# A graph-attention stack: new rows stored from ScalarE's queue, and eleven buffers for the mask rows

## The chip, the cores and the metric

The kernel runs on one core of a Trainium2 chip. Its time is the device time of one execution in microseconds (us). The engines are PE (TensorE, matmul), DVE (VectorE), ACT (ScalarE), POOL (GpSimd) and SP (SyncE, which here only issues DMAs). ACT and POOL can issue DMAs too; the profile writes SPq and ACTq for the queues.

## The reference

Four graph-attention layers work on 3327 nodes with 512 features, over one adjacency matrix with few neighbours per node. Each is preceded by a layer norm and a relu, and added to its input:

```
h = relu(layernorm(x))
v = h @ W                                   # per head
e[i, j] = leaky_relu(s1[i] + s2[j], 0.2)    # s1, s2: scores, linear in v
alpha = softmax over the neighbours j of i
x = x + (alpha @ v)                         # layers 1 and 2: elu(...) first
```

The layers have 8, 4, 1 and 8 heads. The neighbours of a node are the same in all layers.

## The kernel before

The nodes are padded to 3328, 26 tiles of 128. A first stage (until the first gather of layer 0, at 273.46 us) reads the adjacency matrix, makes for every node a list of its neighbours, and ranks the nodes by their number, so that tile 0 has the nodes with the most neighbours (up to 36) and tile 25 those with the fewest (up to 11). The tables idx and twice say, for each tile and each k, the row of the k-th neighbour.

Each layer then has a table in DRAM with one row of 528 numbers per node: v and the scores. Layer 0 reads tabx; layers 1, 2 and 3 read tabs[1], tabs[0], tabs[1], which the layer before fills. In the profile these are all "tab".

**Gathered tiles (class Tile).** Tiles run from 25 down to 0. For each k, an indirect DMA of POOL (gather, L835) brings 128 neighbour rows into a buffer g; four of them make a group, and seven groups can be in flight (LOOK, gpool). For a group, scored adds the scores on DVE (z, L888 and L890) and takes the exponential on ACT (pw, L891); in layer 0 ACT also turns the neighbours' numbers into ranks (idx, L894). group multiplies on DVE (m, L917) and adds up on PE against the identity (bank, L922); with one head, in layer 2, DVE does both (L912). When a tile is complete its row goes through means, added, centre, root, turn, cut, project: DVE, ACT, PE and again PE (pv, L469). Last comes rows: ACT scales the result into v (L476, three buffers), and a DMA stores v in the next layer's table (L993). The pieces of one tile are spread over the steps of the following tiles by later(step, place, piece). The orders of POOL, PE, DVE and ACT are as written; that of SP is chosen by a scheduler when the program is built.

**Dense tiles.** The first tiles have many neighbours, so from layer 1 on they are computed densely, with masks of the adjacency: one tile in layer 1 and two in layer 3 (class Several), nine in layer 2 (class Wholes). These load rows of the table and of the masks through SP (L1230 and L1231 in Several, L1099 and L1101 in Wholes).

**Masks.** The masks are made in layer 0. Mask gathers the adjacency rows of the nine first tiles, turns them on PE, and keep stores them in the DRAM tensor found (L1041), whose rows are in the nodes' old order. Ranked(j), one for each of 26 tiles, brings them into rank order: POOL gathers 128 rows of found, 288 words each, into an SBUF buffer (L835), and SP stores the buffer in masks (L1061). Eight of these stand between the last eight steps of layer 0, and 18 after them. Their buffers are parts of spare, a tile of the first stage that nothing else in layer 0 uses:

```
rows = spare[:, self.j % 3 * n:(self.j % 3 + 1) * n].bitcast(I32)
gather(rows, found, slots(self.j, 0))
```

low, also a tile of the first stage (128 x 3328 words), holds a gathered adjacency row block for Mask earlier in layer 0, and is divided among the buffers of Several (a, e, b, c, v, mk, s) in layers 1 and 3; Wholes uses parts of it in layer 2.

The first gather of a layer waits for all 26 stores of its table.

Of the kernel before, what the change touches and what calls it, by code (L numbers as in the profile page):

```python
# [13 lines left out]
I32 = mybir.dt.int32  # L14
# [4 lines left out]
P = 128  # L19
# [18 lines left out]
ND = max(DENSE)  # L38
# [435 lines left out]
def scaled(nc, pv, rstd, work):  # L474
    v = work.tile([P, ROW], F32, name="v", bufs=3)
    nc.scalar.activation(v.rearrange("p (s n) -> p s n", s=2), pv[:, :, :ROW // 2], AF.Copy, scale=rstd)  # L476
    return v
# [319 lines left out]
def tile_gat_lists(ctx: ExitStack, tc: tile.TileContext, x, adj, ws, avs, out, ident, half, slots, L, low, spare, tabx, tabs):  # L797
# [7 lines left out]
    nc = tc.nc  # L805
# [26 lines left out]
    L, low, spare = [t.rearrange("p a b -> p (a b)") for t in (L, low, spare)]  # L832

    def gather(out_, table, which):
        nc.gpsimd.indirect_dma_start(out=out_, out_offset=None, in_=table,  # L835
                                     in_offset=bass.IndirectOffsetOnAxis(ap=which, axis=0))
# [3 lines left out]
    def scatter():  # L840
        while waiting:
            dst, t, rows = waiting.pop(0)
            nc.gpsimd.indirect_dma_start(out=dst, out_offset=bass.IndirectOffsetOnAxis(ap=slots(t, 0), axis=0),
                                         in_=rows, in_offset=None)

    class Tile:
# [10 lines left out]
        def fetch(self):  # L857

            l, t = self.l, self.t
            i = len(self.groups)  # L860
            k0 = self.k0[i]
            n = (self.k0 + [CAPS[t]])[i + 1] - k0
            g = gpool.tile([P, GROUP, ROW], F32, name="g")
            for q in range(n):
                if l > 0 and k0 + q == 0:
                    nc.sync.dma_start(g[:, 0, :], tabs[l % 2][t * P:(t + 1) * P, :])
                elif l > 0:
                    gather(g[:, q, :], tabs[l % 2], slots(t, k0 + q))
                elif k0 + q == self.own:
                    gather(g[:, q:q + 2, :].rearrange("p q n -> p (q n)"), tabx, slots(t, 0))  # L870
                else:
                    gather(g[:, q, :], tabx.rearrange("r (s n) -> (r s) n", s=2),
                           slots(t, k0 + q + (k0 == 0), twice=True))
            self.groups.append((k0, n, g))
# [115 lines left out]
        def rows(self):  # L990
            if self.W is not None:
                v = scaled(nc, self.pv, self.rstd, work)
                nc.sync.dma_start(tabs[(self.l + 1) % 2][self.t * P:(self.t + 1) * P, :], v)  # L993

        def ends(self, s):

# [54 lines left out]
    class Ranked:  # L1051
# [3 lines left out]
            self.j, self.k0 = j, [0]  # L1055

        def fetch(self):
            n = ND * P // 4
            rows = spare[:, self.j % 3 * n:(self.j % 3 + 1) * n].bitcast(I32)
            gather(rows, found, slots(self.j, 0))  # L1060
            nc.sync.dma_start(masks[:, self.j, :, :].rearrange("s p c -> p s c"),  # L1061
                              rows.rearrange("p (s c) -> p s c", c=wide // 4))
# [269 lines left out]
    for l in range(NL):  # L1332
# [3 lines left out]
        with ExitStack() as c2:  # L1336
# [39 lines left out]
            for s in range(-1, at_end):  # L1376
# [10 lines left out]
                if 0 <= s < len(steps):  # L1387
                    tl, i = steps[s]
# [55 lines left out]
```

## Time and profile before

| | |
|---|---|
| median of 3 runs | 3037.67 us (3028.95 to 3050.73) |
| the profiled execution's own time | 2485.15 us |
| its span, first to last instruction | 2483.4 us |
| busy: PE, DVE, POOL, ACT | 84%, 78%, 69%, 37% |
| granted TensorE clock, mean | 0.944 |
| DMA moved | 599.55 MB, 241 GB/s |
| layer 0, gathers of its own rows | 273.46 to 889.34 us |
| layer 1, first gather | 939.12 us |
| layer 2, first gather | 1495.78 us |
| layer 3, first gather | 1957.66 us |

The profiled execution is 552.5 us shorter than the median of the runs. Durations in this document are those of the profiled execution.

In the lines of the profile "out<-in xN" is N instructions that read "in" and write "out", by the program's names; a group of waits gives us in total, times, longest. A row of the table of stretches gives the length of the stretch, the busy time and number of instructions of PE, PEld (weight load), DVE, ACT and POOL, the granted clock of PE, the DMA engines' mean busy share, and GB/s. A row in order of time gives start, duration, engine, line, operation, tiles, and in brackets the idle time before it and what ended it.

### The profile page before, as it was taken

How to read it: one execution, taken by the hardware profiler on the slowest of the kernel's cores; microseconds unless marked ns; L12 is line 12 of the kernel's file. 1: busy time of each engine (PE TensorE's matmuls, PEld its weight loads, DVE VectorE, ACT ScalarE, POOL GpSimd, SP SyncE). 2: the span in 40 equal slices, each digit the busy share in tenths (PEclk: the TensorE clock that was granted, in tenths of full speed). 3: DMA queues.
4: the chain of work that ended last, by engine and by line, in shares of the span. 5: the costliest groups of instructions: out<-in, count | busy, mean ns of one | idle time of the engine just before them, and what ended most of it. 6: DMA issues, size and time to landing. Idle time of an engine off the chain costs nothing. (4 is left out here: it accounts for less than half of the span.)

```text
span 2483.4 us, 26799 instructions
## 1 busy us (share of the span) xinstructions
PE 2077.1 (84%) x6832; PEld 1161.7 (47%) x6832; DVE 1935.1 (78%) x5004; ACT 910.9 (37%) x2506; POOL 1709.5 (69%) x1700
## 2 busy tenths in 40 slices
PE   3778699999988846999999986869696699999897
PEld 1666345454444423555555543444353454455453
DVE  7988787887777725888888867978979488787776
ACT  4777024343321102434333323433333444333330
POOL 7898467777777756776777746655545377777775
PEclk9888899999999977999999998989898899999999
DMA  6796579999987878887888858867776488888885
GB/s 229 300 304 236 174 240 283 298 289 293 275 269 235 232 182 243 263 248 227 247 259 258 253 150 272 268 197 250 209 227 204 141 254 246 247 249 248 242 242 173
DMA packets 262490, 599.55 MB, mean 241 GB/s; under 512 B 103923, under 2 KB 121331, under 8 KB 257974
## 3 DMA queue, kind: packets, MB, share of 16 engines
q0 software_dynamic: 126128, 438.08, 58.6%
q1 hardware_dynamic: 132454, 152.86, 19.1%
q10 hardware_dynamic: 3744, 6.82, 0.8%
q8 instruction: 55, 0.90, 0.1%
q14 instruction: 109, 0.89, 0.1%
HBM read 547.96 MB, written 49.65 MB: 241 GB/s over the span
## 5 line engine op out<-in xcount | busy, mean ns | idle before, releaser
L922 PE MATMUL bank<-m,ident 128*128 128x512 f32 x2608 | 1202.3, 607 | 131.9 <-DVE m L917 131.2
L917 DVE TENSOR_TENSOR m<-g,pw 128x512 f32<-128x512 f32 x1304 | 810.7, 681 | 138.2 <-ACT pw L891 133.2
L835 POOL DMA_INDIRECT g<-tab,idxb x734 | 697.8, 951 | 281.7 <-issue 170.7
L922 PEld LDWEIGHTS bank<-m,ident 128*128 128x128 f32 x2608 | 482.7, 193 | 711.8 <-issue 345.2
L469 PE MATMUL pv<-w,hT 128*128 128x264 f32 x1664 | 439.0, 419 | 71.0 <-ACT hT L458 41.7
L891 ACT ACTIVATE pw<-z 128x32 f32<-128x32 f32 (+5 forms) x434 | 84.0, 194 | 987.8 <-DVE z L890 987.5
L469 PEld LDWEIGHTS pv<-w,hT 128*128 128x128 f32 x1664 | 336.5, 206 | 173.2 <-ACT hT L458 48.3
L835 POOL DMA_INDIRECT g<-tabx,twiceb x342 | 324.0, 947 | 104.4 <-issue 77.1
L835 POOL DMA_INDIRECT g<-tab,idxa x297 | 283.0, 953 | 148.0 <-issue 81.3
L1138 PE MATMUL whole<-ve,em 128*128 128x512 f32 x468 | 222.0, 623 | 41.0 <-DVE em L1124 38.9
L888 DVE TENSOR_TENSOR z<-g,pw 128x32 f32<-128x32 f32 (+5 forms) x434 | 75.0, 173 | 195.8 <-DMA g<-tab,idxa 88.4
L695 POOL TENSOR_TENSOR key<-a,keys 128x3328 int32<-128x3328 int32 (+1 forms) x29 | 189.4, 6536 | 16.6 <-DVE cand L704 12.9
L912 DVE SCALAR_TENSOR_TENSOR bank<-g,pw,bank 128x512 f32<-128x512 f32 x243 | 183.2, 754 | 6.8
L1138 PEld LDWEIGHTS whole<-ve,em 128*128 128x128 f32 x468 | 90.5, 199 | 151.1 <-issue 91.8
L704 DVE MAX8 cand<-key 128x8 f32<-128x208 int32 x416 | 143.8, 364 | 0.1
L835 POOL DMA_INDIRECT g<-tabx,twicea x99 | 94.4, 954 | 69.6 <-issue 31.3
L451 PE MATMUL pt<-ident,xn 128*128 128x128 f32 x416 | 68.8, 292 | 84.5 <-ACT hT L458 30.9
L451 PEld LDWEIGHTS pt<-ident,xn 128*128 128x128 f32 x416 | 54.3, 150 | 121.5 <-issue 49.4
L1113 ACT ACTIVATE r<-low,mc,b 128x384 f32<-128x384 f32 x78 | 52.6, 674 | 150.1 <-DVE em L1124 115.7
L1247 ACT ACTIVATE r<-low,spare 128x256 f32<-128x256 f32 x208 | 98.9, 476 | 5.1
L432 POOL TENSOR_TENSOR rstd<-ve,half 128x1 f32<-128x1 f32 x52 | 31.9, 615 | 94.8 <-DVE ve L975 60.4
L890 DVE SCALAR_TENSOR_TENSOR z<-z 128x32 f32<-128x32 f32 (+5 forms) x434 | 78.7, 181 | 15.2 <-DVE z L888 0.2
(175 smaller groups left out, 2113.6 us busy)
## 6 DMA issues: line engine op xcount, KB each, us to landing
a<-in_adj SPq DMA_DIRECT2D x25, 1664.0 KB
tab<-v SPq DMA_DIRECT2D x78, 264.0 KB
ve<-tab SPq DMA_DIRECT2D x78, 264.0 KB
g<-tab SPq DMA_DIRECT2D x66, 264.0 KB
tabx<-vx SPq DMA_DIRECT2D x26, 528.0 KB
g<-tab,idxb POOLq DMA_INDIRECT x734, 3.9
low<-tab SPq DMA_DIRECT2D x52, 132.0 KB
room<-tab SPq DMA_DIRECT2D x52, 132.0 KB
```

Of the source, the lines that this page charges most:

```text
L451: nc.tensor.transpose(pt[:, k, :], xn[:, k * P:(k + 1) * P], ident)
L469: nc.tensor.matmul(pv[:, s, :HF + 8], hT[:, k, :], W.w[:, k, s, :], start=(k == 0), stop=(k == KC - 1))
L695: nc.gpsimd.tensor_tensor(key[:, c:c + quarter], a[:, c:c + quarter], keys[:, c:c + quarter], OP.mult)
L704: nc.vector.max(cand[:, g * 8:(g + 1) * 8], key[:, g * SEG:(g + 1) * SEG])
L835: nc.gpsimd.indirect_dma_start(out=out_, out_offset=None, in_=table, in_offset=bass.IndirectOffsetOnAxis(ap=which, axis=0))
L890: nc.vector.scalar_tensor_tensor(z, z, SLOPE, z, OP.mult, OP.max)
L891: nc.scalar.activation(self.wt[:, k0:k0 + n, :H], z, AF.Exp)
L912: nc.vector.scalar_tensor_tensor(acc, v, w, acc, OP.mult, OP.add)
L917: nc.vector.tensor_tensor(m[:, q, :].rearrange("p (s h d) -> p s h d", s=2, d=D), v.rearrange("p s (h d) -> p s h d", d=D), wt[:, k0 + q, ...
L922: nc.tensor.matmul(self.po, ident, m[:, q, :], start=(k0 + q == 0), stop=(k0 + q == K - 1))
L1138: nc.tensor.matmul(tl.po.rearrange("p (s m) -> p s m", s=2), e[:, q * P:(q + 1) * P], v.rearrange("p (s m) -> p s m", s=2)[:, :, :F // 2], ...
L1247: nc.scalar.activation(self.r[:, h, :], self.a[:, g, :], AF.Relu, bias=-1.0, scale=self.b[:, j, g:g + 1])
```

## The change

The store of the new rows is issued by ScalarE instead of SP. The buffers of Ranked are parts of low instead of spare: low has room for 3328 // 288 = 11 of them, where there were three.

```
         def rows(self):
             if self.W is not None:
                 v = scaled(nc, self.pv, self.rstd, work)
-                nc.sync.dma_start(tabs[(self.l + 1) % 2][self.t * P:(self.t + 1) * P, :], v)
+                nc.scalar.dma_start(tabs[(self.l + 1) % 2][self.t * P:(self.t + 1) * P, :], v)
...
         def fetch(self):
-            n = ND * P // 4
-            rows = spare[:, self.j % 3 * n:(self.j % 3 + 1) * n].bitcast(I32)
+            n, many = ND * P // 4, low.shape[1] // (ND * P // 4)
+            i = self.j % many
+            rows = low[:, i * n:(i + 1) * n].bitcast(I32)
             gather(rows, found, slots(self.j, 0))
             nc.sync.dma_start(masks[:, self.j, :, :].rearrange("s p c -> p s c"),
                               rows.rearrange("p (s c) -> p s c", c=wide // 4))
```

## The prediction

> **What bounds the kernel now.** I read the busy line of the page first, then the table of stretches, then the waits by engine, then the instructions in order of time around the one place where both edits meet: the end of layer 0.
>
> ```profile
> PE 2077.1 (84%) x6832; PEld 1161.7 (47%) x6832; DVE 1935.1 (78%) x5004; ACT 910.9 (37%) x2506; POOL 1709.5 (69%) x1700
> ...
> 800.00:890.00 90.00, 77.85 (x200) 37.15 (x201) 59.61 (x148) 14.01 (x50) 68.06 (x73) 0.96 0.82 226
> ...
> 1300.00:1400.00 100.00, 100.00 (x319) 55.16 (x318) 86.90 (x230) 37.97 (x115) 75.62 (x81) 1.00 0.86 260
> ...
> 910.00:915.00 5.00, 0.00 (x0) 0.00 (x0) 0.00 (x0) 0.00 (x0) 2.83 (x3) 0.54 0.66 168
> ```
>
> In the steady stretches POOL issues 81 gathers in 100 us, one per 1.25 us (0.95 busy, 0.30 issue): it is never idle, and layers 0, 1 and 3 go at its pace, PE close behind. The last row is different: from 910 to 935 us PE, DVE and ACT do nothing. That hole is the boundary between layers 0 and 1, and the longest wait of DVE is in it:
>
> ```profile
> DVE z L888 <- DMA g<-tab,idxa: 88.4, 15, 41.5
> ...
> 888.39 0.95 POOL L835 DMA_INDIRECT g<-tabx,twiceb  x1 [0.30 <-issue]
> 889.64 0.94 POOL L835 DMA_INDIRECT spare<-found,idxb  x1 [0.30 <-issue]
> 894.04 0.94 POOL L835 DMA_INDIRECT spare<-found,idxb  x1 [3.46 <-DMA masks<-spare]
> ...
> 929.16 0.95 POOL L835 DMA_INDIRECT spare<-found,idxa  x1 [0.52 <-issue]
> 939.12 0.94 POOL L835 DMA_INDIRECT g<-tab,idxa  x1 [9.01 <-DMA tab<-v]
> ...
> 932.98 0.53 SPq L993 DMA_DIRECT2D tab<-v  x1
> ...
> 869.99 0.70 ACT L476 ACTIVATE v<-pv,rstd 128x528 f32<-128x528 f32 x1 [3.42 <-PE pv L469]
> 872.31 0.20 ACT L891 ACTIVATE pw<-z 128x32 f32<-128x32 f32 x1 [1.63 <-DVE z L890]
> ...
> 896.25 0.18 ACT L891 ACTIVATE pw<-z 128x8 f32<-128x8 f32 x1 [2.71 <-DVE z L890]
> ...
> 906.38 0.70 ACT L476 ACTIVATE v<-pv,rstd 128x528 f32<-128x528 f32 x1 [3.92 <-PE pv L469]
> ```
>
> Layer 0's last own gather goes at 888.39. 19 mask gathers follow; with three buffers each third waits for a store of the masks' rows, so they take 889.64 to 930.1 where 19 x 1.25 = 23.8 us would do. The last new row is ready at 907.08, but its store stands on SP behind the masks' stores and leaves at 932.98. Layer 1's first gather is let go at 939.12.
>
> **What the Trainium skill says.** "DMA: Bandwidth & Descriptors", section "Issuing engines are not separate DMA queues": transfers of all issuing engines end on the same 16 DMA engines, so another queue saves only issue time. By that page, moving the stores gives no bandwidth; what moves is who waits. "Two DMAs through the same engine are not ordered" says that order comes from the completion semaphore, for which the issuing engine waits. The trace agrees in effect: 69 waits of SP for v, 441.8 us in all. The same page, "Anatomy of one DMA": a fixed cost of about 2 us that is mostly completion. Here a tab store took 2.9 and 3.1 us from issue to the gather that needs it at the other two boundaries (1492.91 to 1495.78, 1954.55 to 1957.66). "TensorE: Matmul & The Clock Gate", Part 1, says the clock halves when PE idles and returns with work; the granted clock is 0.54 and 0.50 in the hole above.
>
> **The change, part by part.** PE, DVE and POOL keep their instructions in the same order, save that 26 gathers write low instead of spare. SP loses 78 stores, ScalarE gains 78, each right after its v. The waits that the changed program gives these stores decide the sum. All direct DMAs, of SP and ScalarE alike, take their completion semaphores from one set of eight, and each waits until the last user of its semaphore has completed. For a store now on ScalarE that user is mostly a transfer of SP, and ScalarE stands in order behind the wait.
>
> 1. *Eleven buffers.* The gathers need not wait in threes: 889.64 + 19 x 1.25 = 913.4 for the first gather of layer 1, if its table is there. That alone would be 939.12 - 913.4 = 25.7 us. DMA share in 890 to 935 us is 0.49 to 0.88, 29 us of full share in 45; compressed it fits barely, so up to 4 us of it may come back as slower landings.
>
> 2. *The second-last tab store waits for the eighth masks store.* Its v is ready at 870.7. The eighth mask gather is issued at 889.64 by POOL, which does not depend on ScalarE here (the buffers it needs were read before 870). Its two predecessors took 5.8 and 7.1 us from gather to store; its own store left at 895.3 in the trace, and the next stores completed in 2.7 to 3.1 us: done at 898 to 900, I take 899. So ScalarE is held from 870.7 to 899, and behind it stand the five remaining exponentials of layer 0 (872.31 to 896.25), for which DVE and then PE wait.
>
> 3. *The catch-up.* 17 rows (4+4+4+4+1) remain. PE takes 7.03 us for 16 matmuls at full clock, so 34 take 15; with 2.5 us for a halved clock at the start it ends at 899.5 + 17.5 = 917. From PE's end to the end of the last v the trace has 8.3 us (898.74 to 907.08), plus the wait before: v at 926.
>
> 4. *The last tab store waits for the last masks store*: gather 26 at 912.1, stored 3.2 to 7 us later and complete 3 us after that, 919 to 922. That is before 926 and costs nothing; it would decide if step 3 were 5 us faster.
>
> 5. Store at 926.1, landing 3.0: the first gather of layer 1 at 929.1 instead of 939.12. **Gain 10 us** (7 if it lands as slowly as the 6.1 us of before, 13 if PE keeps its clock). SP's part behind it (scores, values, masks of layer 1) waits for the same store, so DVE starts earlier by the same amount; POOL has seven groups of lookahead, and layer 1 moves as a whole.
>
> 6. *ScalarE's cost.* A direct DMA on its queue takes 0.334 us (the x loads of the first stage): 78 x 0.334 = 26 us, and up to 0.2 more each for its own v to end. ScalarE waits 2.6 us on average before its exponentials in layer 1 (290.5 us in 110 waits), so most is covered. Bounds: 0 and 42 us; I take 2, at layer ends.
>
> 7. *Other waits on shared semaphores.* In layers 1 and 2 nearly every store waits for an SP load. By the program's order that load stands 81 to 442 instructions earlier, and a layer has 5.7 to 7.2 per us: 14 us or more, against 3.3 to 6.3 us for a load to land. The exception, the last store of layer 1, waits for a small score load issued some 10 us before it (1480 to 1484, against 1492.9). I take 0; bounds 0 and 52 us (1 us each for 52).
>
> 8. *SP freed.* Loads no longer stand behind v. Only ScalarE's wait for ve (11.6 us in 6) shows loads late; three of them, 5.2 us, stand near a tab store. Gain 0 to 5, I take 1. The other two boundaries gain nothing: SP issued those stores 0.03 us after v.
>
> Sum: -10 + 2 - 1 = -9 us. Profiled execution: 2485.15 - 9 = 2476. The median of the runs shown is 3037.67, 552.5 us above the profiled execution, and nothing in the profile says where these lie. The gain carries over as 9 us, or as 11 if everything stretches alike. I predict 3028.
>
> **Rivals.**
> - *A, the above*, 50 in 100: 3028, own range 3013 to 3045.
> - *B, the full gain*: ScalarE isn't held at the eighth masks store (v comes later in unprofiled runs, or the catch-up is faster), and the whole 25.7 us stay: 2459 profiled, 3012 by difference, 3006 in proportion. For it: POOL's pure pace. Against it: the waits of step 2, which the program contains. 18 in 100, half of it beyond 1%.
> - *C, more*: if the missing 552.5 us are longer round trips, the ring of three costs more there: 19/3 rounds of 12 instead of 6 us is 76 us against about 30, a gain of 45: 2993. Against it: unknown. 14 in 100.
> - *D, slower*: one mechanism, ScalarE held in layers 1 and 2 by semaphores of SP loads, with z, exponential and product behind it. At 1 us for each of 52 stores it is 52 - 9 = +43: 2528 profiled, 3081. It cancels the gain from 0.17 us each and passes 1% from 0.75. For it: ScalarE is in every group's chain. Against it: step 7. 18 in 100.
>
> **How the numbers follow.** About 1% (30 us) is what a measurement of this kernel tells from no change. Faster: 9 of B, 14 of C, 2 of A make 0.25. Slower: 16 of D and 1 of A make 0.17. The rest is 0.58. The range, 2990 to 3065, holds A, B and nearly all of C, and leaves out most of D.
>
> **What would show it.** In the changed profile: mask gathers 1.25 us apart; ScalarE idle from about 870 to 899 between v and its store, with PE idle beside it; layer 1's first gather near 929; no wait over 1 us ahead of a store in layers 1 and 2. The forecast is wrong if ScalarE passes the second-last store at once (then B) or if DVE's waits for pw grow by tens of us in layers 1 and 2 (then D).

## The result, and the profile after

The changed kernel takes 3047.23 us (median of 14 runs, 3037.62 to 3062.81), the kernel before beside it 3025.88 us (14 runs): a ratio of 1.007, 95% interval 1.0048 to 1.0091. It is slower by 21 us; the forecast was 3028 us, with a gain of 9.

The kernel before took 2487 us in two of the five sets of runs below (the first kind) and 2993 to 3055 us in the other three (the second kind); within a set its executions lie within 1.7% of each other, and each set ran on a chip of its own. The profile that the prediction read was of the first kind, the runs of this comparison of the second. The profile of the changed kernel is of the second kind too (3058.75 us, span 3057.0), so it is read against a second profile of the kernel before, e0_before (span 3040.1). From the page of the changed kernel, its busy line and the chain that ended last, by engine:

```profile
PE 2252.4 (74%) x6832; PEld 1233.5 (40%) x6832; DVE 1930.9 (63%) x5004; ACT 918.0 (30%) x2506; POOL 1714.2 (56%) x1700
...
PE 35%; DVE 18%; issue 16%; another core or an unknown queue 12%; ACT 8%; DMA 6%; POOL 3%; ACTq 0%; DVEq 0%; SPq 0%; POOLq 0%
```

POOL is busy 56% of the span, not 69%: it no longer sets the pace. 12% of the chain lies behind a releaser that the profile cannot name. The same appears among the waits of the changed kernel (us in all, times, longest):

```profile
POOL g L835 <- issue: 491.7, 1305, 16.1
...
DVE m L917 <- ACT pw L891: 340.2, 171, 28.7
...
ACT v L476 <- remote: 119.7, 9, 30.0
```

"remote" is a wait for which no instruction or transfer ended at the right time. DVE's longest wait for an exponential was 4.5 us in the profile that the prediction used; here it is 28.7, and it stands at the place that the prediction spoke of (e0_before has one of 24.0 us, but in layer 3). Instructions of POOL, PE, ACT and DVE there, in order of time, in the changed kernel:

```profile
1069.77 0.21 ACT L894 ACTIVATE idxb<-g 128x4 int32<-128x4 f32 x1
1070.54 0.95 POOL L835 DMA_INDIRECT g<-tabx,twiceb  x1 [0.30 <-issue]
1071.48 3.72 PE L469 MATMUL pv<-w,hT 128*128 128x264 f32 x16
1071.80 0.95 POOL L835 DMA_INDIRECT low<-found,idxb  x1 [0.30 <-issue]
1073.05 0.95 POOL L835 DMA_INDIRECT low<-found,idxb  x1 [0.30 <-issue]
...
1094.88 0.95 POOL L835 DMA_INDIRECT low<-found,idxa  x1 [0.85 <-issue]
1100.02 0.70 ACT L476 ACTIVATE v<-pv,rstd 128x528 f32<-128x528 f32 x1 [30.04 <-remote]
1100.75 0.33 ACTq L993 DMA_DIRECT2D tab<-v  x1
1101.36 1.88 DVE L917 TENSOR_TENSOR m<-g,pw 128x512 f32<-128x512 f32 x3 [28.71 <-ACT pw L891]
...
1134.20 0.95 POOL L835 DMA_INDIRECT g<-tab,idxa  x1 [38.37 <-DMA tab<-v]
```

The 19 mask gathers that follow layer 0's own now go without a break, from 1071.80 to 1094.88, as forecast. But ScalarE is not held at the second-last store: that leaves at 1100.75, as soon as its v has ended. All 78 stores of this profile leave 0.03 us after their v. It is v itself that comes 30 us late, although PE's product for it ended near 1075.2. In e0_before, with the ring of three:

```profile
1065.70 0.95 POOL L835 DMA_INDIRECT spare<-found,idxb  x1 [0.30 <-issue]
1067.86 0.95 POOL L835 DMA_INDIRECT spare<-found,idxb  x1 [1.21 <-DMA masks<-spare]
1073.40 0.95 POOL L835 DMA_INDIRECT spare<-found,idxb  x1 [4.60 <-DMA masks<-spare]
...
1077.03 0.70 ACT L476 ACTIVATE v<-pv,rstd 128x528 f32<-128x528 f32 x1 [6.34 <-PE pv L469]
...
1114.62 0.95 POOL L835 DMA_INDIRECT g<-tab,idxa  x1 [8.27 <-DMA tab<-v]
```

POOL has to stop for stores, for 4.60 us among others, and v follows PE's product at once. Two stretches of 25 us among the mask gathers, first of the changed kernel, then of e0_before (columns as in the prediction):

```profile
1075.00:1100.00 25.00, 3.64 (x9) 1.34 (x8) 0.00 (x0) 0.00 (x0) 15.41 (x17) 0.62 0.71 189
```

```profile
1080.00:1105.00 25.00, 21.18 (x55) 10.81 (x54) 13.77 (x39) 4.07 (x13) 11.37 (x12) 0.93 0.59 157
```

With eleven buffers PE ends its last 3.6 us of work and then POOL works alone; DVE and ACT do nothing for 25 us. With three, PE, DVE and ACT finish layer 0 under the mask gathers.

An engine that has finished an instruction raises a counter, its completion semaphore, and an engine that needs the result waits for a count. The trace records when TensorE's counter rises, and that shows what "remote" is here. In e2_buffers (below), where PE's product for v ended near 1076.9 and v waits from 1072.5 to 1102.85, the rises are at 1080.22, 1085.83, and then at 1102.83, 1102.87, 1102.91, 1102.95 and 1103.00: two completions come through singly during the row of gathers, and five at once 5 us after the last mask gather ended. v waits for one of them. Its only other wait was for a store three rows earlier, and that had landed at 978.9. The Trainium skill, "Perfetto Trace Analysis", section "Tensor Engine Instruction (MATMUL, LD_WEIGHTS)", says that the end of a matmul in a profile is an estimate, and that the update of the semaphore is pushed, and then made known to all engines, after it. The trace agrees that the two differ: here by some 26 us.

Such bursts (two rises or more within 0.06 us of each other) are 117 in e0_before and 103 in the changed kernel, and 4 in the profile that the prediction read. The larger ones were taken from seven traces with gathers 1.25 us apart (four rises or more after over 3 us without one, 9 to 30 gathers in an unbroken row ahead): 129 of them. Each comes after a stop of POOL, 2.8 to 6.3 us after the last gather was issued, and the later the longer the row: a straight line gives 1.82 us + 0.139 us for each gather of the row (correlation 0.94). It looks as if each gather took 1.39 us of something, while POOL issues one every 1.25 us, and as if TensorE's signals came through only when the backlog is worked off.

### The profile page after: what moved, and what is told of

It is laid out like the page before. It is cut to its first block, busy times and chain, and to the rows that moved or that the text cites. A ratio compares the mean times of both kernels' runs of the same rounds, so it can differ in the third digit from the quotient of the medians.

```text
span 3057.0 us, 26770 instructions
## 1 busy us (share of the span) xinstructions
PE 2252.4 (74%) x6832; PEld 1233.5 (40%) x6832; DVE 1930.9 (63%) x5004; ACT 918.0 (30%) x2506; POOL 1714.2 (56%) x1700
## 4 chain that ended last, share of the span: by engine, by line
PE 35%; DVE 18%; issue 16%; another core or an unknown queue 12%; ACT 8%; DMA 6%; POOL 3%; ACTq 0%; DVEq 0%; SPq 0%; POOLq 0%
PE bank L922 23%; PE pv L469 7%; DVE m L917 6%; DVE bank L912 3%; POOL g L835 3%; DMA vx<-in_x 3%; PE whole L1282 2%; ACT r L1248 1%; PE pi L786 1%; ACT v L476 1%; DMA g<-tab,idxa 1%; DVE prod L409 1%; ACT pw L891 1%; PE whole L1139 1%
## 5 line engine op out<-in xcount | busy, mean ns | idle before, releaser
L922 PE MATMUL bank<-m,ident 128*128 128x512 f32 x2608 | 1330.1, 658 | 353.9 <-DVE m L917 223.1
L917 DVE TENSOR_TENSOR m<-g,pw 128x512 f32<-128x512 f32 x1304 | 811.1, 682 | 573.5 <-ACT pw L891 340.2
L922 PEld LDWEIGHTS bank<-m,ident 128*128 128x128 f32 x2608 | 529.7, 211 | 1015.2 <-issue 629.5
L476 ACT ACTIVATE v<-pv,rstd 128x528 f32<-128x528 f32 x78 | 54.1, 694 | 291.6 <-remote 119.7
L1259 ACT ACTIVATE spare<-room,low 128x64 f32<-128x64 f32 x208 | 57.8, 336 | 201.7 <-remote 101.1
L458 ACT ACTIVATE hT<-pt 128x512 f32<-128x512 f32 x104 | 61.4, 590 | 143.9 <-PE pt L451 42.5
L1282 PE MATMUL whole<-spare,low 128*128 128x130 f32 x416 | 67.3, 301 | 48.1 <-issue 47.9
```

The source lines that it names most:

```text
L917: nc.vector.tensor_tensor(m[:, q, :].rearrange("p (s h d) -> p s h d", s=2, d=D), v.rearrange("p s (h d) -> p s h d", d=D), wt[:, k0 + q, ...
L922: nc.tensor.matmul(self.po, ident, m[:, q, :], start=(k0 + q == 0), stop=(k0 + q == K - 1))
L1282: nc.tensor.matmul(dst, e[:, h, q * P:(q + 1) * P], mov, start=False, stop=(j == NT - 1), skip_group_check=True)
```

## The experiments

Theories at the start: H, ScalarE held at its stores by shared semaphores in all layers; B, only the hold at the end of layer 0; M, the eleven buffers cost. From the second set on, W: TensorE's signals don't come through while gathers follow one another, and the ring of three was what broke their row.

**First set: which part** (kernel before: 3055.41 us, 48 runs). e0_before is the kernel before. e1_stores has only the first edit, e2_buffers only the second, and e3_layer0 both, with

```
+                queue = nc.scalar if self.l == 0 else nc.sync
```

for the store. Expected of the four, in this order:

> The kernel before, profiled a second time beside the others, to have a trace at the pace of the timed runs. Both theories: a span of 3015 to 3050 us, clock about 0.87, POOL's waits for the instruction stream (issue) near 490 us as in the changed kernel. What they differ in: theory H (ScalarE held at its stores) expects ScalarE's waits put down to no known source ahead of new rows or of casts into low or spare near 0 here, against 120 + 101 + 82 us in the changed kernel; theory B (the boundary alone) expects them about alike in both and the difference of 21 us inside the stretch from the last gather of layer 0 to the first of layer 1.

> The stores of new rows on ScalarE's queue, the masks' rows in three buffers as before. Theory H (ScalarE held, in all layers, until the last user of a shared completion semaphore is done): ratio to before 1.010 to 1.020, as the cost is all here and no buffers pay it back. Theory B (only the hold ahead of the second-last store of layer 0 costs): with three buffers the eighth masks store comes as late as before, so the cost is the whole of it, 1.005 to 1.010. Theory M (the eleven buffers are what costs): 0.995 to 1.002.

> Eleven buffers for the masks' rows, the stores of new rows on SP as before. Theory H: 0.990 to 0.998, a gain of 8 to 25 us at the end of layer 0, as forecast for the full gain. Theory B: the same. Theory M (buffers cost: SP's last new row stands behind more masks stores, or low is wanted by something else): 1.004 to 1.010.

> Eleven buffers; ScalarE's queue for the stores of layer 0 alone, those of layers 1 and 2 on SP again. Theory H: two thirds of the stores are no longer held, so 0.993 to 1.002. Theory B: the hold at the end of layer 0 is untouched, so 1.005 to 1.009, as the changed kernel.

Measured: e0_before 3041.78 us, one run. e1_stores 1.0015 (0.9996 to 1.0033): moving the stores costs nothing that can be told. e2_buffers 1.0061 (1.0037 to 1.0086): the buffers alone cost what the change costs. e3_layer0 1.0036 (1.0016 to 1.0056). H and B, both taken from the prediction, fall by e1_stores, where they wanted 1.010 and 1.005 or more, and by the 0.03 us between v and store above; H also by e0_before, which has "remote" waits too, 623 us of them where the changed kernel has 494. M stands; e3_layer0 lies below what B wanted and above what H wanted, and its interval overlaps that of e2_buffers. In e2_buffers ScalarE issues no store of new rows and v waits just as long:

```profile
1102.85 0.70 ACT L476 ACTIVATE v<-pv,rstd 128x528 f32<-128x528 f32 x1 [30.33 <-remote]
```

The place is plain in the stages of the profiles (us; layer 0 from its first gather to the first of layer 1, and so on; one execution each):

| kernel | mask buffers | v of the second-last tile | layer 0 | layer 1 | layer 2 | layer 3 |
|---|---|---|---|---|---|---|
| e0_before | 3 | 1077.0 | 842.5 | 758.1 | 489.2 | 678.2 |
| e1_stores | 3 | 1080.4 | 842.9 | 745.6 | 489.1 | 679.7 |
| e2_buffers | 11 | 1102.8 | 863.2 | 759.3 | 485.8 | 675.4 |
| e3_layer0 | 11 | 1094.8 | 856.8 | 757.5 | 485.7 | 678.3 |
| changed | 11 | 1100.0 | 858.5 | 757.2 | 485.7 | 680.0 |
| f1_after | 11 | 1107.4 | 864.3 | 743.8 | 489.0 | 675.5 |
| f2_buffers | 11 | 1103.7 | 862.9 | 759.9 | 485.1 | 682.9 |
| f3_pause | 11, POOL pauses | 1074.4 | 837.8 | 766.6 | 485.8 | 680.6 |

With three buffers layer 0 takes 842.5 and 842.9, with eleven 856.8 to 864.3: 14 to 22 us more. The five ratios with eleven buffers and no pause make it 11 to 21 us in the whole time. (In f1_after it is the cast hT, one step ahead of v, that is held for 28.7 us, by the same row of mask gathers.) Layer 1 varies by 23 us from one execution to the next without regard to the buffers, so single profiles tell nothing there.

**Second set: a pause, a pace, six buffers** (kernel before: 2487.29 us, 28 runs). e4_pause is the changed kernel with

```
             gather(rows, found, slots(self.j, 0))
+            if self.j >= 8 and self.j % 3 == 1:
+                for _ in range(4):
+                    nc.gpsimd.memset(spare[:, :3 * n], 0.0)
```

e5_pace is the changed kernel, e6_pace_b the kernel before, with a fill after every gather of all layers:

```
+    idle = spool.tile([P, 256], F32, name="idle", bufs=1)
     def gather(out_, table, which):
         nc.gpsimd.indirect_dma_start(...)
+        nc.gpsimd.memset(idle, 0.0)
```

e7_six is the changed kernel with many = 6.

> The changed kernel, and after every third of the 19 mask gathers that follow layer 0's own gathers POOL fills an unused buffer four times (about 3.2 us), a pause like that which the ring of three buffers forces. Theory W (TensorE's completion signals don't come through while POOL issues gathers one after another, and come through some us after it stops; the ring's waits are such stops): the wait ahead of the second-last new row falls from 30 us to under 8, layer 1 starts about as in the kernel before, ratio 0.995 to 1.003, although POOL has 20 us more to do. Rival S (the stores of the masks' rows, sent in a burst, are what costs): the pauses only delay layer 1 further, 1.007 to 1.014.

> The changed kernel, and after every gather of all layers POOL fills a small buffer (128x256, an estimated 0.30 us), so that gathers go at most every 1.45 to 1.55 us in place of 1.25. Theory W, in the form that a gather needs 1.4 us of something that TensorE's signals need too: the backlog never forms, the waits on no known source go nearly away, and the kernel gets faster though POOL does more: 0.85 to 0.95. Rival S: POOL's time only grows, 1.02 to 1.10.

> The same filling after every gather in the kernel before (three buffers, stores on SP). Theory W: as fast as the changed kernel with it or up to 25 us slower, since with paced gathers the eleven buffers should bring what was forecast of them; 0.85 to 0.96. Rival S: 1.02 to 1.10.

> The changed kernel with six buffers for the masks' rows in place of eleven. Theory W: POOL stops for a store after at most six mask gathers, for some 2 us, so the wait ahead of the second-last new row is between that of three and of eleven, 6 to 20 us, ratio 0.998 to 1.004. Rival S: six stores in flight are a burst too, 1.004 to 1.008.

Measured: 1.0018 (1.0009 to 1.0027), 1.0873 (1.0856 to 1.0889), 1.0892 (1.0875 to 1.0908) and 1.0016 (1.0008 to 1.0024). This set was of the first kind: 2 to 4 bursts in a trace, no "remote" wait, POOL setting the pace, so a fill only slows it. On W it says nothing. But it is the situation that the prediction had reckoned with, and e7_six, though it has six buffers and not eleven, shows its steps one by one:

```profile
870.50 0.70 ACT L476 ACTIVATE v<-pv,rstd 128x528 f32<-128x528 f32 x1 [4.39 <-PE pv L469]
...
899.17 0.33 ACTq L993 DMA_DIRECT2D tab<-v  x1
899.55 0.20 ACT L891 ACTIVATE pw<-z 128x32 f32<-128x32 f32 x1 [28.35 <-DMA masks<-low]
...
925.75 0.70 ACT L476 ACTIVATE v<-pv,rstd 128x528 f32<-128x528 f32 x1 [3.92 <-PE pv L469]
926.49 0.33 ACTq L993 DMA_DIRECT2D tab<-v  x1
...
932.29 0.95 POOL L835 DMA_INDIRECT g<-tab,idxa  x1 [15.90 <-DMA w<-in_w]
```

Here ScalarE is held at the second-last store, to 899.17, and the first gather of layer 1 goes at 932.29 in place of 939.12; the releaser named is the transfer that landed last by the profile. Then layers 1, 2 and 3 take 565.8, 465.3 and 527.2 us in place of 556.7, 461.9 and 525.8 (from the first gathers 1498.09 and 1963.36, and the span of 2490.6): the 6.8 us are given back twice. e4_pause is held at the same store, from 871.67 to 897.17, and loses alike: 564.2 and 465.5 us in layers 1 and 2.

**Third set: the same on the kind of the result** (kernel before: 3034.89 us, 59 runs). f1_after is the changed kernel, f2_buffers is e2_buffers, f3_pause is e4_pause, f4_pace is e5_pace.

> The changed kernel again, beside runs of the kernel before on the same chip. The last four kernels ran on a chip on which the kernel before took 2487 us in place of 3026 to 3055, with no bursts in TensorE's completion signals. If the chip is like that one: the boundary between layers 0 and 1 some 7 us earlier than before, 12 us lost in layers 1 and 2, 1.001 to 1.003. If it is like the one of the result: 1.005 to 1.009.

> Eleven buffers, stores of new rows on SP. On a chip of 2487 us: the last store of layer 0 waits on SP only for the last masks rows, layer 1's first gather at 916 to 922 in place of 939, and nothing lost in layers 1 and 2: 0.990 to 0.994. On a chip of 3026 us or more: 1.004 to 1.009 as before (theory W).

> The changed kernel with a pause of POOL of about 3.2 us after every third of the last mask gathers. On a chip of 3026 us or more, theory W: the wait ahead of the second-last new row falls from 30 us to under 8 and the ratio to 0.995 to 1.003; rival S (the burst of masks stores): 1.007 to 1.014. On a chip of 2487 us: 1.001 to 1.003, as measured.

> The changed kernel with a small fill of POOL after every gather of all layers, which makes a gather take 1.5 us in place of 1.25. On a chip of 3026 us or more, theory W (a gather needs about 1.4 us of what TensorE's signals need too): 0.87 to 0.97, the bursts in TensorE's signals gone; rival S: 1.02 to 1.10. On a chip of 2487 us: 1.085 to 1.09, as measured.

Measured: 1.006 (1.0034 to 1.0085), 1.0041 (1.0019 to 1.0063), 1.0038 (1.0017 to 1.006) and 0.9249 (0.9196 to 0.9302). The last fits W and not S, which wanted 1.02 or more: POOL does more and the kernel is 7.5% faster. W's forecast that the bursts would be gone did not come true, though: there are 155. POOL's row of gathers in f4_pace, 1.44 us apart:

```profile
700.47 0.95 POOL L837 DMA_INDIRECT g<-tabx,twiceb  x1 [0.16 <-issue]
701.43 0.33 POOL L839 MEMSET idle<- 128x256 f32 x1
701.91 0.95 POOL L837 DMA_INDIRECT g<-tabx,twiceb  x1 [0.16 <-issue]
```

The pause does at its place what W said: in f3_pause v comes at 1074.41 and layer 1 starts at 1110.75, 19 to 31 us earlier than in the five profiles with eleven buffers and no pause, though POOL has some 20 us more to do before that. v starts 2.7 us after POOL's first pause begins:

```profile
1070.78 0.95 POOL L835 DMA_INDIRECT low<-found,idxb  x1 [0.30 <-issue]
1071.72 3.47 POOL L1064 MEMSET spare<- 128x864 f32 x4
...
1074.41 0.70 ACT L476 ACTIVATE v<-pv,rstd 128x528 f32<-128x528 f32 x1 [9.21 <-PE bank L922]
...
1110.75 0.95 POOL L835 DMA_INDIRECT g<-tab,idxa  x1 [0.16 <-issue]
```

The wait ahead of v is 9.21 us (under 8 was expected), and its releaser is PE again. The buffers are still eleven and still parts of low, so neither their place nor their number holds v by itself: what differs is the break in POOL's row. Nor are the stores of the masks' rows, S's cause, denser where v is held: they leave every 2.8 us from 1080 to 1097 in the changed kernel, every 2.1 us from 1079 to 1108 in e0_before. In the whole time the pause brings less than this: 1.0038 is just past the 0.995 to 1.003 expected, and its interval overlaps that of f1_after. Layer 1 takes 766.6 us in that profile; whether the pauses cause that, or it is layer 1's usual spread, stays open.

**Fourth set: a need of 1.4 us, or any break** (kernel before: 2992.77 us, 7 runs). g1_short and g2_long are the changed kernel with fills of 128x128 and 128x448; g3_pace_b is e6_pace_b.

> The changed kernel with a shorter fill after every gather (128x128, an estimated 0.20 us): a gather every 1.31 us. Theory W with a need of 1.41 us per gather (1.25 plus the 0.165 us by which the release came later for each gather of a run): still under the need, the backlog grows by 0.1 us per gather in place of 0.165, so most of the holds stay: 0.96 to 1.00 on a chip of 3026 us or more. Rival P (any break between gathers lets the signals through, whatever its length): 0.85 to 0.93, less than with the longer fill since POOL does less. On a chip of 2487 us both: 1.02 to 1.04.

> The same with a longer fill (128x448, an estimated 0.49 us): a gather every 1.60 us. Theory W with a need of 1.41: no holds are left to remove, POOL alone sets the pace, so slower than with 1.44 us by up to 0.16 us for each of some 1500 gathers: 0.93 to 1.00 on a chip of 3026 us or more. Rival Q (the need is far more than 1.44 us and the shorter fill freed the signals in part only): 0.85 to 0.91. On a chip of 2487 us both: 1.14 to 1.19.

> The kernel before (three buffers, stores on SP) with the fill of 128x256 after every gather, for a chip of 3026 us or more: with paced gathers the signals come through, so the eleven buffers and the stores on ScalarE have only what was forecast of them, up to 10 us either way: 0.920 to 0.930 where the changed kernel with the same fill had 0.925. On a chip of 2487 us: 1.089, as measured.

Measured: 0.9872 (0.9827 to 0.9917), 0.9695 (0.9647 to 0.9742), 0.9153 (0.9104 to 0.9203). With the changed kernel of the result and f4_pace (of the third set) these make a row, each ratio against its own kernel before; "remote" is summed over the waits that the profile lists:

| gather every | ratio | "remote" waits, us | bursts |
|---|---|---|---|
| 1.25 us (changed) | 1.007 | 494 | 103 |
| 1.33 us (g1_short) | 0.987 | 538 | 91 |
| 1.44 us (f4_pace) | 0.925 | 211 | 155 |
| 1.44 us (g3_pace_b, three buffers) | 0.915 | 145 | 158 |
| 1.60 us (g2_long) | 0.970 | 0 | 2 |

A fill of 0.22 us between gathers is not enough (P falls); at 1.60 us the holds are all gone, and POOL alone is slower than with 1.44 (Q falls). g3_pace_b lies a little below its 0.920 to 0.930. At 1.44 the bursts are many but short: the silences of more than 3 us ahead of a burst sum to 112 us in f4_pace and 60 in g3_pace_b, against 224 to 335 in the seven profiles at 1.25 (142 at 1.33, 4 at 1.60). The pace at which the holds end lies between 1.44 and 1.60 us. The 1.39 us worked out from the bursts would have left none at 1.44, so as a fixed need of every gather it is too small, or the need varies. In g2_long DVE's waits for the exponential are short again:

```profile
DVE m L920 <- ACT pw L894: 88.5, 284, 2.5
```

**Fifth set: the change without the hold** (kernel before: 2486.68 us, 9 runs). h1_pace and h2_pace_b are e5_pace and e6_pace_b, h3_pace_150 the kernel before with a fill of 128x320.

> The changed kernel with the fill of 128x256 after every gather (1.44 us each), beside the next two on one chip. On a chip of about 3000 us: 0.920 to 0.930.

> The kernel before with the same fill. If the change is worth nothing or a small loss once the hold is gone (ScalarE's cost in layer 1, about 9 us on the chip of 2487 us, against 7 us gained at the boundary), within 0.005 of h1_pace on the same chip; if the eleven buffers still cost, as some bursts are left at 1.44 us, lower than h1_pace by 0.005 to 0.012.

> The kernel before with a fill of 128x320 (an estimated 0.39 us, a gather every 1.50 us). Theory W with a need of about 1.4 us: fewer bursts than with 1.44 us, POOL 0.06 us slower for each of 1559 gathers (94 us at most): 0.90 to 0.93 on a chip of about 3000 us; 1.11 to 1.13 on one of 2487 us.

Measured: 1.0865 (1.0847 to 1.0883), 1.089 (1.0872 to 1.0908), 1.1134 (1.1119 to 1.1149). The set was of the first kind again, so it doesn't answer what was open. What it tells is that with POOL paced the change is worth 0.25% or less there (1.0865 against 1.089, intervals touching). What the change is worth with the hold gone on the kind of the result stays open: f4_pace and g3_pace_b, 1% apart, were measured in different sets.

The fastest version for the kind of the result is g3_pace_b, the kernel before with a paced POOL: 8.5% faster. Where the kernel before takes 2487 us, the same version is 8.9% slower.

## Why the prediction was wrong

- *Step 1, eleven buffers let the mask gathers go 1.25 us apart*: right in the runs of the result (1071.80 to 1094.88 for 19); no run of the first kind has eleven buffers without a pause or a fill. That this brings layer 1 forward is seen only where TensorE's signals aren't held, with six buffers (e7_six).
- *Step 2, ScalarE held from 870.7 to 899*: measured in e7_six, 871.2 (v's end) to 899.17. In the runs of the result there is no such hold; the second-last v is itself too late, and by then the masks store is done.
- *Steps 3 to 5, v at 926, the first gather at 929.1*: v ends at 926.45 and the gather goes at 932.29 in e7_six. The gain at the boundary was 6.8 us, the 7 named for a slow landing.
- *Steps 6 and 7, ScalarE's cost, 2 + 0 us*: mis-sized. In e7_six layers 1 and 2 are 9.1 and 3.4 us longer, 12.5 us in place of 2 (11.1 in e4_pause), well within the bounds given (0 to 42 and 0 to 52). With 6.8 us gained in place of 10, the sum is then -6.8 + 12.5 - 1 = +4.7 in place of -9, and e7_six and e4_pause measure +0.16% and +0.18%, 4 us. It is not step 7: in e7_six and e4_pause each of the 52 stores of layers 1 and 2 leaves 0.03 us after its v. What is left is step 6, as 52 stores take 17 us on ScalarE, or the buffers in low and SP's new order; no run of the first kind has one edit alone, so this stays open.
- *Step 8, SP freed, 1 us*: too small to be seen in any run.
- *The step that failed*: "nothing in the profile says where these lie. The gain carries over as 9 us, or as 11". The 552.5 us between the profile and the runs were taken for an amount that the change doesn't touch. They go with the holds of TensorE's signals: paced at 1.44 us per gather the kernel before takes 2739 us on the second kind (g3_pace_b) and 2711 on the first (e6_pace_b), 28 us apart in place of 506 (2993 against 2487). The holds last as long as POOL's row of gathers does, and making a row longer is just what the eleven buffers do. The term "eleven buffers, -25.7 us" has the opposite sign there: +14 to +22 us in layer 0, and +12 to +19 us by the ratios of e2_buffers and f2_buffers (0.0061 x 3055, 0.0041 x 3035).
- *The rivals*: D, the slower one, had the sign, but not the cause (e1_stores 1.0015). C asked what the missing 552.5 us would do to the ring of three, which was the right question, but took them for longer round trips, which would have made the ring dearer. B named what came, a later v in the runs and ScalarE not held at the store, but took it for the full gain of 25.7 us. That a wait for a buffer could do good was in none of them.
- *What would show it*: of the four signs named, the first and the last came (mask gathers 1.25 us apart; no wait over 1 us ahead of a store in layers 1 and 2), and the second by half: PE idle beside a long wait of ScalarE, but the wait lies ahead of v and not between v and its store. The third, layer 1's first gather near 929, did not. "DVE's waits for pw grow" came as well, by 72 us (340.2 against 268.6 in e0_before), but 28.7 of it is one wait at the end of layer 0.
- *A reading that says less than it was taken for*: SP's 69 waits for v are waits for ScalarE's result, not for the completion of a transfer. A wait of the latter sort is ScalarE's 28.35 us for "masks<-low" in e7_six.

## What to carry to other kernels

Where the profile is 18% shorter than the timed runs, it is a profile of another situation: before summing steps on it, ask what in the runs is bound that isn't bound there, and whether the change feeds that. A wait for a buffer can be a break that other engines live on; before taking it away, look at who moves in that gap. In a kernel that lives on indirect gathers, "remote" waits and bursts of semaphore rises after POOL's stops are the sign to try a slower pace of gathers, in the setting where the kernel is to run, as the same fill was worth -8.5% and +8.9%.

## What the runs showed of the hardware

- In the second kind, while POOL issued gathers 1.25 us apart, completions of TensorE were held, ahead of one v for some 26 us, and then came 0.04 us apart, 2.8 to 6.3 us after the last gather was issued. Through what the gathers and TensorE's signals get into each other's way isn't shown, nor whether VectorE's and ScalarE's signals are held too: in e0_before and e2_buffers there is one burst of theirs after more than 3 us, but these traces have only some 60% of their rises on record (1351 of ScalarE's where the first kind has 2284), against 82% of TensorE's (1737 of 2106).
- The hold appears in three sets of runs of five, each time in all profiles with gathers 1.25 to 1.44 us apart, and in no profile of the other two. What makes a set one or the other isn't known; each set ran on another chip and no chip had two sets, so it may be the chip, and that isn't shown.
- A POOL fill of 128x128, 128x256 and 128x448 words took 0.22, 0.33 and 0.49 us. 0.14 us of it goes into the 0.30 us that lie between two gathers anyway, so a gather came every 1.33, 1.44 and 1.60 us.
